# Mixture of experts on one core: one-hot rows from PSUM for seven experts, an expert's outputs ahead of the slot numbers three experts on

## The chip, the cores and the metric

The kernel runs on one core of a Trainium2 chip. The metric is the device time of one execution in microseconds (us); less is better. Compared are medians of several executions.

## The reference

The input `x` is 2 x 2048 tokens of 256 numbers. Four blocks follow each other, each a layer norm, a layer and a residual sum:

```
x = x + linear_attention(layernorm(x))      # 16 heads of 16
x = x + ffn(layernorm(x))                   # mixture of 8 experts
x = x + windowed_attention(layernorm(x))    # causal, a window per head, gates
x = x + ffn(layernorm(x))                   # the same weights once more
```

The change lies in `ffn`, which is computed twice:

```
probs = softmax(xf @ gate_w.T)              # 4096 tokens x 8 experts
scores = route(probs)                       # threshold 0.9, then the best 512 tokens of each expert
y = sum over e of scores[:, e] * (gelu(xf @ w1[e].T) @ w2[e].T)
```

Each expert keeps at most 512 tokens, so the kernel computes an expert on 512 gathered rows alone.

## The kernel before

Tokens lie in 32 tiles of 128. While the attention blocks run, `router` writes every normalized row and its 8 probabilities to DRAM (`rows_a`, and `rows_b` in the second pass) and the running sum `x` to `mid` (in the second pass `out_rows`). Then `experts` works alone on the core, once behind each attention.

`experts` first finds each expert's threshold by bisection. Then it gives each kept token a slot. A slot's number is split into a part `hi` (which of 128 rows) and a part `lo` (which of four blocks). For an expert `e` four steps turn this into token numbers:

- `columns_of(e)`: two small VectorE (DVE) products (L1013 into `olo`, L1017 into `olw`) and one on ScalarE (ACT, L1016 into `olw`).
- `rows_of(e)`: two one-hot tiles `ohi` of 16 token tiles x 128, one a half. For `e < SHARED` both operands are bf16 in SBUF (L1028, with `hi2` written by L1078); for other experts the counting numbers are fp32 in PSUM (`iota_ps`, L1034).
- `tokens(e)`: 32 small matmuls on TensorE (PE, L1045) sum `ohi` against `olw` into `w_ps`, 16 for each half; then three small DVE steps (L1049, L1050, L1052) write the token numbers `idx[e]`.
- `gather(n)`: the next `n` blocks of 128 rows are fetched by indirect DMAs that GpSimd (POOL) issues (L1070, into `xe`).

The loop over experts (L1097) then does for `e`: eight transposes of the four blocks on PE (`transposed`, L247), two copies of the result to SBUF (ACT L251; the second on DVE, L249), the first product (`h_ps`, L1110, 8 matmul records), Gelu on ACT (L1112), and for each of the four blocks the second product (`y_ps`, L1123, in two PSUM buffers), its scaling on DVE (L1126 into `y`) and an indirect DMA on POOL that adds 128 rows into `mid` or `out_rows` (L1127). Inside the loop also stand `columns_of`, `rows_of` and `tokens` of expert `e + 3`: between the Gelu and the second product.

PE, ACT and DVE work through their instructions in the order in which the code is written. POOL's order is fixed by dependencies: gathers in their order, an expert's additions behind the last gather written before them (`follow`), gathers behind the additions written before them. An expert's additions also wait until those of the expert before have landed. The `gather` tuple at the end of the loop says how many blocks are fetched behind each expert's additions; together with `gather(2)` for `e == 0` all 32 blocks are fetched. SyncE (SP) has no transfer in this loop. `xe` has four buffers, `ohi` four, `y` eight.

Of the kernel before, what the change touches and what calls it, by code (L numbers as in the profile page):

```python
# [30 lines left out]
E, F = 8, 256  # L31
# [23 lines left out]
CENTERS, SCALES = (-6.0, -3.0, -1.5, -0.5), (0.25, 0.5, 1.0, 1.0)  # L55
STEPS = [0.25 * 4.0**-i for i in range(12)]
SIGN = 2.0**20
SHARED = 3
ROUND = 1.5 * 2.0**23 * GT


# [73 lines left out]
def hybrid_kernel(ctx: ExitStack, tc: tile.TileContext, x, wq, wk, wv, wo, wqk, bqk, wgate, bgate, wproj, bproj,  # L135
# [13 lines left out]
    def part(t, name):  # L149
        o, n = at[name]  # L150
        return t[:, o : o + n]
# [9 lines left out]
    def con(name):  # L161
        return part(cst, name)
# [78 lines left out]
    def transposed(pool, psum, xn, copies=None, n=GT):  # L241

        xnT = pool.tile([P, NC, GW], F32, name="xnT", tag="xnT")[:, :, 0 : n * P]
        for c in range(NC):
            pt = psum.tile([P, GW], F32, name="xnT_ps", tag="mm")[:, 0 : n * P]
            for i in range(n):
                nc.tensor.transpose(pt[:, i * P : (i + 1) * P], xn[:, i, c * P : (c + 1) * P], ident)  # L247
            if c and copies is None:
                nc.vector.tensor_copy(xnT[:, c, :], pt)  # L249
            else:  # L250
                nc.scalar.copy(xnT[:, c, :], pt)  # L251
        return xnT
# [640 lines left out]
    def experts(acc, name, rows, scores):  # L893
        score, over = scores
        with ExitStack() as st:
            pool = st.enter_context(tc.tile_pool(name=f"mx_{name}", bufs=2))
            one = st.enter_context(tc.tile_pool(name=f"mo_{name}", bufs=1))
            mm = st.enter_context(tc.tile_pool(name=f"mm_{name}", bufs=4, space=PSUM))
# [98 lines left out]
            hi = one.tile([P, E, NT], BF16, name="hi")  # L997
            hi2 = one.tile([P, SHARED, NT, 2], BF16, name="hi2")
            lo = one.tile([P, E, NT], BF16, name="lo")

            def of(t, e):
                return t.rearrange("p (t e) -> p e t", e=E)[:, e]
# [7 lines left out]
            def columns_of(e):  # L1010

                olo = pool.tile([P, NT, GT], BF16, name="olo", tag="olo")
                nc.vector.tensor_tensor(olo, lo[:, e].unsqueeze(2).to_broadcast([P, NT, GT]),  # L1013
                                        part(sel, "places").unsqueeze(1).to_broadcast([P, NT, GT]), ALU.is_equal)
                columns[e] = olw = pool.tile([P, NT, 2, GT], BF16, name="olw", tag="olw")
                nc.scalar.activation(olw[:, :, 0, :], olo, AF.Copy, scale=con("within"))  # L1016
                nc.vector.tensor_tensor(olw[:, :, 1, :], olo, part(sel, "tile").rearrange("p (t l) -> p t l", l=GT),  # L1017
                                        ALU.mult)
# [3 lines left out]
            def rows_of(e, halves=range(2)):  # L1022

                for b in halves:
                    ohi = pool.tile([P, half, P], BF16, name="ohi", tag="ohi", bufs=4)
                    at_b = slice(b * half, (b + 1) * half)
                    if e < SHARED:
                        nc.vector.tensor_tensor(  # L1028
                            ohi.rearrange("p t (a b) -> p t a b", b=2),
                            hi2[:, e, at_b].unsqueeze(2).to_broadcast([P, half, P // 2, 2]),  # L1030
                            iota.rearrange("p (a b) -> p a b", b=2).unsqueeze(1).to_broadcast([P, half, P // 2, 2]),
                            ALU.is_equal)
                    else:
                        nc.vector.tensor_tensor(ohi, iota_ps.unsqueeze(1).to_broadcast([P, half, P]),  # L1034
                                                hi[:, e, at_b].unsqueeze(2).to_broadcast([P, half, P]), ALU.is_equal)
                    ones.setdefault(e, []).append(ohi)

            def tokens(e):

                olw = columns.pop(e)  # L1040
                w_ps = sm.tile([P, 2, GT], F32, name="w_ps", tag="sm")
                for b, ohi in enumerate(ones.pop(e)):
                    for t in range(half):
                        n = b * half + t
                        nc.tensor.matmul(w_ps.rearrange("p w l -> p (w l)"), ohi[:, t, :],  # L1045
                                         olw[:, n].rearrange("p w l -> p (w l)"), start=(n == 0), stop=(n == NT - 1))

                row = pool.tile([P, GT], F32, name="row", tag="row")
                nc.vector.scalar_tensor_tensor(row, w_ps[:, 0, :], 0.0, con("spare"), ALU.is_equal, ALU.mult)  # L1049
                nc.vector.scalar_tensor_tensor(row, w_ps[:, 0, :], -1.0, row, ALU.add, ALU.add)  # L1050
                idx[e] = one.tile([P, GT], I32, name=f"idx{e}")
                nc.vector.scalar_tensor_tensor(idx[e], w_ps[:, 1, :], float(P), row, ALU.mult, ALU.add)  # L1052
# [12 lines left out]
            def gather(n):  # L1065

                for e, b in blocks[:n]:
                    if b == 0:
                        xes[e] = pool.tile([P, GT, XR], F32, name="xe", tag="xe", bufs=4)
                    read = nc.gpsimd.indirect_dma_start(  # L1070
                        out=xes[e][:, b, :], out_offset=None, in_=rows[:, :],
                        in_offset=bass.IndirectOffsetOnAxis(ap=idx[e][:, b : b + 1], axis=0))
                    follow(read, reads[-1:] + added)
                    reads.append(read)
                del blocks[:n]

            for e in range(SHARED):
                nc.vector.tensor_scalar(hi2[:, e], of(up, e).unsqueeze(2).to_broadcast([P, NT, 2]), ROUND, 1.0 / GT, ALU.subtract,  # L1078
# [10 lines left out]
            for e in range(1, 3):  # L1089
# [3 lines left out]
                    los(slice(2, E))  # L1093
                tokens(e)
                gather(GT)
            columns_of(3)
            for e in range(E):  # L1097
                xe = xes.pop(e)
                adds = []

                for blocks_in in ((range(GT),) if e + 1 < E else (range(GT - 1), range(GT - 1, GT))):
                    at0, n = blocks_in[0], len(blocks_in)
                    xT = transposed(pool, mm, xe[:, at0 : at0 + n, :], None, n)
                    if e == 0:
                        rows_of(3)
                    hT = pool.tile([P, F // P, GW], F32, name="hT", tag="hT")
                    for f in range(F // P):
                        h_ps = mm.tile([P, GW], F32, name="h_ps", tag="mm")
                        for c in range(NC):
                            nc.tensor.matmul(h_ps[:, 0 : n * P], w1_sb[:, e, c, f * P : (f + 1) * P], xT[:, c, :],  # L1110
                                             start=(c == 0), stop=(c == NC - 1))
                        nc.scalar.activation(hT[:, f, 0 : n * P], h_ps[:, 0 : n * P], AF.Gelu)  # L1112
                    if e + 3 < E:
                        if e:
                            columns_of(e + 3)
                            rows_of(e + 3)
                        tokens(e + 3)
                        if e == 0:
                            gather(2)
                    for b in blocks_in:  # L1120
                        y_ps = yp.tile([P, D], F32, name="y_ps", tag="y")
                        for f in range(F // P):
                            nc.tensor.matmul(y_ps, hT[:, f, (b - at0) * P : (b - at0 + 1) * P], w2_sb[:, e, f, :],  # L1123
                                             start=(f == 0), stop=(f == F // P - 1))
                        y = pool.tile([P, D], F32, name="y", tag="y", bufs=8)
                        nc.vector.tensor_scalar(y, y_ps, xe[:, b, D + e : D + e + 1], None, ALU.mult)  # L1126
                        add = nc.gpsimd.indirect_dma_start(  # L1127
                            out=acc[:, :], out_offset=bass.IndirectOffsetOnAxis(ap=idx[e][:, b : b + 1], axis=0),
                            in_=y, in_offset=None, compute_op=ALU.add)

                        for other in adds:
                            tc.declare_no_dep(add.ins, other.ins, reason="rows of one expert's slots differ")
                        for other in added:
                            tc.add_manual_dep(add.ins, other.ins.name, landed, reason="sums of the expert before")
                        follow(add, reads[-1:])
                        adds.append(add)
                added = adds
                gather((2, 3, 3, 3, 3, 3, 1, 0)[e])
            return added


# [585 lines left out]
```

## Time and profile before

| what | value |
|---|---|
| median of 11 executions | 907.49 us (903.46 to 909.62) |
| the profiled execution | 907.75 us |
| its span, first to last instruction | 905.6 us |
| mean granted TensorE clock | 0.913 |
| busy, whole span | PE 84%, DVE 72%, POOL 48%, ACT 43% |
| expert loop, first pass | first gather at 331.79 us, end of the last addition's issue at 443.0 us |
| expert loop, second pass | first gather at 789.65 us, end of the last addition's issue at 901.15 us |

The profile is one execution. Times in its rows count from the first instruction. A timeline row has the start, the duration, the engine (PEld is the weight load of PE), the source line, the operation, the tiles written and read, how many instructions are merged, and in brackets how long the engine was idle before and what ended the idle time. A row of stretches has the length, the busy time of each engine with its number of instructions, the granted TensorE clock, the DMA engines' share and GB/s. A row of instruction groups has the line, the operation, the shapes, the count, then busy time and mean nanoseconds, then idle time before. A row of waits has who waited for whom, the total, the number of times, and the longest.

### The profile page before, as it was taken

Reading aid. Unit: us, or ns where it says so; the run is one execution under the profiler, and the core shown is the slowest. Engines: PE = TensorE matmul, PEld = TensorE weight load, DVE = VectorE, ACT = ScalarE, POOL = GpSimd, SP = SyncE. Lnnn points to the kernel's source line nnn. Section 1 sums busy time; section 2 is a strip of 40 time slices with the busy share of each in tenths; the row PEclk is TensorE's granted clock in tenths of the full one; section 3 lists DMA queues with packets and bytes.
Section 4 is the critical chain, followed back from the end, with each engine's and each line's share of the span. In section 5 each row is a group of like instructions: output and inputs, shape, how many; then the busy total and the mean of one; then the engine's idle time right before and its main releaser. Section 6 shows DMA issues by size and latency. Waiting matters only on the chain.

```text
span 905.6 us, 17491 instructions
## 1 busy us (share of the span) xinstructions
PE 756.5 (84%) x6520; PEld 503.7 (56%) x6520; DVE 649.0 (72%) x1665; ACT 387.5 (43%) x1117; POOL 438.7 (48%) x506
## 2 busy tenths in 40 slices
PE   8999999999999327887588999999999993268785
PEld 5577677676677214554345666665656662145453
DVE  6778778678668776652369898888988887856621
ACT  3545545544444331111145576665665762411111
POOL 1233325235235126778543655563655442157786
PEclk8999999999999557999799999999999996569987
DMA  9830101101102113545662023123031212025554
GB/s 310 234 109 6 49 3 47 48 1 49 49 1 96 29 28 74 77 74 81 122 178 63 27 60 109 49 60 105 14 102 56 54 60 65 7 78 77 78 77 63
DMA packets 63996, 65.01 MB, mean 72 GB/s; under 512 B 7244, under 2 KB 60521, under 8 KB 63913
## 3 DMA queue, kind: packets, MB, share of 16 engines
q1 hardware_dynamic: 49945, 44.66, 16.2%
q0 software_dynamic: 12992, 18.42, 12.6%
q8 instruction: 51, 0.84, 0.4%
q10 hardware_dynamic: 976, 0.84, 0.3%
q14 instruction: 32, 0.26, 0.1%
HBM read 26.47 MB, written 27.56 MB: 60 GB/s over the span
## 4 chain that ended last, share of the span: by engine, by line
PE 22%; DVE 18%; issue 4%; ACT 3%; POOL 3%; DMA 1%; POOLq 0%; SPq 0%; DVEq 0%; ACTq 0%
PE tk_ps L1197 5%; PE y_ps L1123 3%; PE wo_ps L1430 2%; PE xnT_ps L247 2%; DVE ohi L1034 2%; PE pt_ps L1395 2%; POOL out_rows L1127 2%; DVE ln_stats L218 2%; DVE wa_xn L226 2%; PE pj_ps L1452 1%; DVE og L1325 1%; DVE s L1287 1%; PE wqk_ps L1204 1%; ACT wpr L1386 1%; PE sa_ps L1365 1%
## 5 line engine op out<-in xcount | busy, mean ns | idle before, releaser
L251 ACT COPY xnT<-xnT_ps 128x512 f32<-128x512 f32 (+2 forms) x73 | 39.0, 563 | 125.9 <-PE xnT_ps L247 125.9
L223 POOL TENSOR_TENSOR ln_rstd<-ln_rstd,cst_parts 128x4 f32<-128x4 f32 (+3 forms) x35 | 34.7, 992 | 114.3 <-DVE ln_rstd L222 77.2
L1123 PE MATMUL y_ps<-w_sb,hT 128*128 128x256 f32 x256 | 69.7, 421 | 7.2 <-DVE y L1126 5.7
L1110 PE MATMUL h_ps<-xnT,w_sb 128*128 128x512 f32 (+2 forms) x144 | 67.3, 615 | 9.8 <-ACT xnT L251 9.3
L1126 DVE TENSOR_SCALAR y<-y_ps,xe 128x256 f32<-128x256 f32 x64 | 30.5, 483 | 58.9 <-PE y_ps L1123 54.7
L523 POOL TENSOR_TENSOR a_sb<-a_raw,cst_first 128x512 f32<-128x512 f32 x32 | 41.1, 1284 | 60.8 <-ACT a_raw L522 60.8
L525 DVE TENSOR_TENSOR a_sb<-s_ps,cst_first 128x512 f32<-128x512 f32 x96 | 60.0, 680 | 8.0 <-PE s_ps L511 8.0
L1123 PEld LDWEIGHTS y_ps<-w_sb,hT 128*128 128x128 f32 x256 | 50.3, 208 | 23.1 <-DVE y L1126 8.9
L218 DVE BATCH_NORM_STATS2 ln_stats<-x 128x6 f32<-128x256 f32 x128 | 53.4, 417 | 7.1 <-DMA x<-in_x 3.3
L1397 ACT COPY pt<-pt_ps 128x256 f32<-128x256 f32 (+3 forms) x94 | 42.0, 468 | 37.1 <-PE pt_ps L1395 36.7
L1127 POOL DMA_INDIRECT out_rows<-y,idx x32 | 50.6, 1582 | 14.9 <-issue 6.6
L1127 POOL DMA_INDIRECT mid<-y,idx x32 | 50.4, 1576 | 14.5 <-DVE y L1126 6.5
L1197 PE MATMUL tk_ps<-wt_sb,xnT 128*128 128x432 f32 x128 | 52.8, 539 | 0.5 <-ACT xnT L251 0.5
L1070 POOL DMA_INDIRECT xe<-rows_a,idx x32 | 31.4, 981 | 41.1 <-DVE idx L1052 29.9
L1070 POOL DMA_INDIRECT xe<-rows_b,idx x32 | 31.3, 978 | 41.1 <-DVE idx L1052 29.9
L1110 PEld LDWEIGHTS h_ps<-xnT,w_sb 128*128 128x128 f32 x144 | 27.9, 211 | 40.5 <-issue 22.7
L1386 ACT ACTIVATE wpr<-sn_ps,negm 128x128 f32<-128x128 f32 x128 | 45.8, 375 | 0.0
L1395 PE MATMUL pt_ps<-cst_parts,wpr 128*128 128x128 f32 x280 | 44.3, 282 | 1.3 <-ACT wpr L1386 1.0
L1112 ACT ACTIVATE hT<-h_ps 128x512 f32<-128x512 f32 (+2 forms) x36 | 19.8, 550 | 59.0 <-PE h_ps L1110 58.9
L1034 DVE TENSOR_TENSOR ohi<-iota_ps,hi 128x2048 bf16<-128x2048 f32 x20 | 44.8, 2280 | 0.0
L1395 PEld LDWEIGHTS pt_ps<-cst_parts,wpr 128*128 128x128 f32 x280 | 31.1, 140 | 24.2 <-issue 5.6
L1045 PE MATMUL w_ps<-olw,ohi 128*128 128x8 bf16 x512 | 17.7, 167 | 31.0 <-DVE ohi L1028 13.6
(260 smaller groups left out, 2097.1 us busy)
## 6 DMA issues: line engine op xcount, KB each, us to landing
ks<-tk SPq DMA_DIRECT2D x21, 280.0 KB
rows_a<-xr SPq DMA_DIRECT2D x7, 528.0 KB
rows_b<-xr SPq DMA_DIRECT2D x7, 528.0 KB
x<-in_x SPq DMA_DIRECT2D x7, 512.0 KB
mid<-x SPq DMA_DIRECT2D x7, 512.0 KB
x<-mid SPq DMA_DIRECT2D x7, 512.0 KB
out_rows<-x SPq DMA_DIRECT2D x7, 512.0 KB
w_sb<-in_w1t SPq DMA_DIRECT2D x1, 2048.0 KB
```

Of the source, the lines that this page charges most:

```text
L218: nc.vector.bn_stats(self.stats[:, i, :], self.xin[:, i, :])
L523: nc.gpsimd.tensor_tensor(a, raw, causal, ALU.mult)
L525: nc.vector.tensor_tensor(a, s_ps[j], causal, ALU.mult)
L1034: nc.vector.tensor_tensor(ohi, iota_ps.unsqueeze(1).to_broadcast([P, half, P]), hi[:, e, at_b].unsqueeze(2).to_broadcast([P, half, P]), AL ...
L1070: read = nc.gpsimd.indirect_dma_start(out=xes[e][:, b, :], out_offset=None, in_=rows[:, :], in_offset=bass.IndirectOffsetOnAxis(ap=idx[e][ ...
L1110: nc.tensor.matmul(h_ps[:, 0 : n * P], w1_sb[:, e, c, f * P : (f + 1) * P], xT[:, c, :], start=(c == 0), stop=(c == NC - 1))
L1123: nc.tensor.matmul(y_ps, hT[:, f, (b - at0) * P : (b - at0 + 1) * P], w2_sb[:, e, f, :], start=(f == 0), stop=(f == F // P - 1))
L1127: add = nc.gpsimd.indirect_dma_start(out=acc[:, :], out_offset=bass.IndirectOffsetOnAxis(ap=idx[e][:, b : b + 1], axis=0), in_=y, in_offse ...
L1197: nc.tensor.matmul(ps, self.xnT[:, c, i * P : (i + 1) * P], wt_sb[:, c, :], start=(c == 0), stop=(c == NC - 1))
L1386: nc.scalar.activation(self.pr[:, o : o + w], src, AF.Exp, bias=self.negm[:, h : h + 1], accum_out=self.den[:, h : h + 1])
L1395: nc.tensor.transpose(ps[:, n, :], self.pr[:, (o + n) * P : (o + n + 1) * P], ident)
L1397: (nc.vector.tensor_copy if engine else nc.scalar.copy)(pt[:, skip:w, :], ps[:, skip:w, :])
```

## The change

Three things are edited. `SHARED` falls from 3 to 1: `hi2` and the bf16 form of `rows_of` stay for expert 0 alone. `columns_of(3)` leaves the place ahead of the loop and `rows_of(3)` and `tokens(3)` the middle of expert 0: all three stand behind expert 0's additions, and expert 0's second copy of the transposed rows goes from DVE to ACT. For later experts `columns_of(e + 3)` and the first half of `rows_of(e + 3)` stand ahead of the first product, and the second half and `tokens(e + 3)` behind the additions of `e`. `gather(2)` inside expert 0 is gone: its additions stand behind the first twelve gathers, and four gathers follow them in place of two.

```diff
-SHARED = 3
+SHARED = 1
...
-            columns_of(3)
             for e in range(E):
                 xe = xes.pop(e)
                 adds = []
 
                 for blocks_in in ((range(GT),) if e + 1 < E else (range(GT - 1), range(GT - 1, GT))):
                     at0, n = blocks_in[0], len(blocks_in)
-                    xT = transposed(pool, mm, xe[:, at0 : at0 + n, :], None, n)
-                    if e == 0:
-                        rows_of(3)
+                    xT = transposed(pool, mm, xe[:, at0 : at0 + n, :], None if e else "scalar", n)
+                    ahead = e + 3 if e + 3 < E else None
+                    if ahead and e:
+                        columns_of(ahead)
+                        rows_of(ahead, [0])
...
                         nc.scalar.activation(hT[:, f, 0 : n * P], h_ps[:, 0 : n * P], AF.Gelu)
-                    if e + 3 < E:
-                        if e:
-                            columns_of(e + 3)
-                            rows_of(e + 3)
-                        tokens(e + 3)
-                        if e == 0:
-                            gather(2)
                     for b in blocks_in:
...
                 added = adds
-                gather((2, 3, 3, 3, 3, 3, 1, 0)[e])
+                if ahead:
+                    if e == 0:
+                        columns_of(ahead)
+                    rows_of(ahead, range(2) if e == 0 else [1])
+                    tokens(ahead)
+                gather((4, 3, 3, 3, 3, 3, 1, 0)[e])
```

## The prediction, made before the changed kernel was run

> **What bounds the kernel now.** I read the page for where the experts lie, then the stretches of the expert loop, POOL's waits, the timeline, and last the clock by window. All numbers are of the first pass; the second repeats it within a microsecond (the loop takes 111.2 and 111.5 us). The stretches are cut where an expert's first addition begins, the last two here those of experts 3 and 4:
>
> ```profile
> 365.30:377.90 12.60, 10.08 (x65) 6.58 (x65) 8.17 (x13) 2.07 (x4) 9.23 (x7) 0.95 0.52 85
> 377.90:390.50 12.60, 11.02 (x65) 7.05 (x65) 7.90 (x13) 2.07 (x4) 9.30 (x8) 0.86 0.49 75
> 390.50:402.80 12.30, 9.49 (x65) 6.18 (x65) 7.79 (x13) 2.07 (x4) 9.26 (x7) 1.00 0.50 75
> 402.80:414.20 11.40, 10.32 (x42) 6.73 (x41) 3.74 (x8) 1.78 (x3) 9.23 (x8) 1.00 0.51 72
> ```
>
> POOL is busy 9.3 us of each, and every one of its issues is followed by 0.30 us, so seven take 11.4 us: experts 4 to 6 run at POOL's own pace. Experts 1 to 3 take 12.3 to 12.6, because POOL waits for `y`:
>
> ```profile
> POOL mid L1127 <- DVE y L1126: 6.5, 6, 1.7
> ```
>
> The timeline has an expert without number work (expert 5), which gives the bare chain, and the release of expert 0's additions:
>
> ```profile
> 345.19 5.81 PE L1110 MATMUL h_ps<-xnT,w_sb 128*128 128x512 f32 x8 [2.61 <-ACT xnT L251]
> 352.64 0.95 POOL L1070 DMA_INDIRECT xe<-rows_a,idx  x1 [3.71 <-DVE idx L1052]
> 355.38 0.48 DVE L1126 TENSOR_SCALAR y<-y_ps,xe 128x256 f32<-128x256 f32 x1 [0.38 <-issue]
> 355.17 1.04 PE L247 MATMUL xnT_ps<-cst_parts,xe 128*128 128x128 f32 x8
> 404.44 1.04 PE L247 MATMUL xnT_ps<-cst_parts,xe 128*128 128x128 f32 x8
> 410.90 0.48 DVE L1126 TENSOR_SCALAR y<-y_ps,xe 128x256 f32<-128x256 f32 x1 [4.62 <-PE y_ps L1123]
> 413.49 0.48 DVE L1126 TENSOR_SCALAR y<-y_ps,xe 128x256 f32<-128x256 f32 x1 [0.38 <-DMA xe<-rows_a,idx]
> ```
>
> To be seen: from the first transpose to the end of the first `y` 6.94 us, to the end of the last 9.53. Expert 1's transposes start (355.17) before expert 0's last `y` is done, since expert 3's one-hot rows were made beside expert 0's `h`.
>
> **The change part by part.** The DVE's groups price the rows:
>
> ```profile
> L1034 DVE TENSOR_TENSOR ohi<-iota_ps,hi 128x2048 bf16<-128x2048 f32 x10 | 22.4, 2280 | 0.0
> L1028 DVE TENSOR_TENSOR ohi<-hi,cst_sel 128x2048 bf16<-128x2048 bf16 x6 | 7.1, 1217 | 0.0
> ```
>
> *SHARED 3 to 1.* Experts 1 and 2 get a pair of 4.47 us (two of 2.28, overlapping) in place of 2.35: +2.12 each; the two `hi2` steps go (-0.2). Expert 1's pair runs 332.13 to 336.60; 0.6 for 16 matmuls and 0.55 for three small steps give `idx` at 337.8, against 337.32 before. That is only +0.5, because before DVE read `w_ps` 1.4 us after the modelled end of its matmuls (2.6 us for expert 2), while for expert 0 it was 0.04. Expert 2's pair then ends at 342.8, its matmuls at 343.4, and expert 0's transposes follow at half clock (four of 0.215 and 0.3): copy 344.55 to 345.1, `h` at 345.2. Before it was 345.19, since the copies stood behind `idx` and `columns_of(3)`. I take 0. Bounds: +2.6 if the late reading is added again; -2.0 if the clock, now fed by transposes right ahead of `h`, rises one 3.41 us window earlier than at 349.46. The middle of this last, -1.0, goes into expert 0 below.
>
> *Both copies on ACT for expert 0:* nothing; ACT is idle there, and the second copy ends at 346.0, before its matmul at 346.9. Without that slack it costs its own 0.58. *ACT's `olw` ahead of Gelu:* nothing; `olo` is there 2.1 us behind the transposes, `olw` at 2.55, the first `h` at 3.4. DVE's first half (2.28) lies under `h` and ends 1.7 us before `y`.
>
> *Expert 0's additions behind twelve gathers.* POOL waited until 352.64 for expert 3's numbers and put two gathers ahead of the additions (355.14). Now the additions start with `y`, at about 353.5, and all four gathers come behind them. The sum of POOL's work is the same, and the 1.6 us are lost again if the numbers come late, and they do.
>
> *Expert 3's numbers behind expert 0's outputs.* DVE's last `y` ended at 355.86; it is not sooner for want of `w_ps`, because `y` also waits for Gelu (351.63); less the 1.0 above it is 354.9. Then 0.5 (`olo`, `olw`), 4.47 (the pair), 0.6 (matmuls): expert 1's transposes, behind them on PE, start at 360.5 in place of 355.17. POOL has issued expert 0's four additions (7.5) by then and its gathers wait for `idx`, with expert 1's additions queued behind. Expert 1's first addition comes 7.2 after its transposes (6.94 and 0.26 to POOL): 367.7, against 365.34.
>
> *The second half behind `y`.* For experts 1 to 4 a period is now 9.53 to the last `y`, 2.28 for the half, 0.6 for 16 matmuls, then the next transposes: 12.4 us. Before, both halves stood in the same chain, partly under `h`, at 12.0 to 12.6. So the moved work frees POOL's wait for `y`, but puts its price between two experts. No DMA is moved but the gathers, and SP has none here. POOL's 11.4 fits into the period: it is no longer the pace.
>
> *The clock.* PE's gap per expert is now in one piece: from the last `y_ps` (8.85 behind the transposes) to 12.4, 3.5 us with only 32 tiny matmuls in it. Such a gap decides the clock (its column is the third from the end):
>
> ```profile
> 359.70:363.11 3.41, 2.25 (x38) 1.68 (x37) 2.58 (x4) 0.89 (x2) 2.80 (x3) 1.00 0.59 69
> 363.11:366.53 3.42, 3.42 (x10) 2.71 (x9) 0.97 (x2) 0.00 (x0) 2.75 (x3) 0.50 0.54 118
> 397.25:400.66 3.41, 2.31 (x38) 2.09 (x38) 1.58 (x1) 0.84 (x2) 2.50 (x4) 1.00 0.55 91
> 400.66:404.07 3.41, 2.08 (x10) 1.50 (x9) 1.60 (x6) 0.00 (x0) 2.17 (x2) 1.00 0.32 79
> ```
>
> A window with 2.25 us of modelled PE time, half of it the tiny matmuls, was followed by half clock for 3.41 us, one with 2.31 was not. A window with 3.5 us of gap in or around it lies well below both, so I take one cold window in nearly every period from expert 1 to 5. It begins in the gap and covers about 2.2 us of the next transposes and `h`, which run at half speed: +1.1 us (bounds 0.5 to 1.7, a window less its part in the gap, halved).
>
> [...]
>
> *Sum for a pass.* Expert 1's first addition: 367.7 + 1.2 = 368.9. Four periods of 12.4 + 1.1: expert 5's at 422.9, against 414.20: +8.7. From there both kernels have POOL's pace (11.4), and expert 7's first addition waits 4.6 us for the landing of expert 6's last (issued 431.27, next 435.87), so the end moves with expert 5: +8.7. Two passes: +17.4 us on the profiled 907.75, which lies 0.26 above the median: 925.
>
> **The rivals.** *Warm clock:* the same chain without cold windows. Expert 1 at 367.7, expert 5 at 367.7 + 4 x 12.4 = 417.3: +3.1 a pass, 914. For it: POOL's idle before shows only some experts with a cold window. Against: the longer gap.
>
> *Faster, POOL set free:* the gain that `y` ahead of the numbers could have. If POOL never waits for `y`, experts 1 to 5 follow at 11.4: 365.3 + 4 x 11.4 = 410.9 against 414.2, -3.3 a pass, 901. It decides only if expert 1's transposes start by 358.1 (365.34 - 7.2), that is 2.2 us behind expert 0's last `y`, where the pair alone takes 4.47; and if a period then falls to 11.4, where the chain has 12.4.
>
> *No difference:* POOL covers all of it, because the two kernels' periods are alike (12.4 and 12.5) and expert 1 comes in time: 907.5. The 5.3 us of expert 1 speak against it.
>
> *Colder:* late reading at the start (transposes of expert 1 at 362.0), four windows of 3.41 in a period (13.65), one more cold window of 1.5 behind: 362.0 + 8.4 + 54.6 = 425.0, +10.8, and 1.5: +12.3 a pass, 932.
>
> **How the numbers follow.** Forecast (cold, 925) 0.63; warm (914) 0.20; colder (932) 0.10; faster (901) 0.04; none 0.03. Low end: warm clock and the clock's early rise in full (expert 1's transposes at 359.4, expert 5 at 416.2): +2.0 a pass, 911.7. High end: the colder case, 932. Outside lie the faster, the unchanged, and part of the colder and warm cases. About 0.2% (1.8 us) is what a measurement of this kernel can tell from no change: faster 0.04, within 0.03, slower 0.93.
>
> **What would show each step.** Right: in the timeline expert 1's transposes at about 360 behind `w_ps`, DVE's pair between expert 0's last `y` and them; 13 to 14 us between first additions of experts 1 to 5 and POOL waiting for `y` 2 us each time; granted clock in the loop well below 0.86; `h` at 345 as before. Wrong: expert 1's transposes before 358; `w_ps` L1045 not waiting for `ohi` L1034; POOL without idle time between experts; or a period of 12.4 at full clock, which gives the warm case.

## The result and the profile after

The kernel after takes 928.5 us (median of 12 runs, 925.7 to 931.5), the kernel before beside it 906.5 us (46 runs): 2.4% slower, ratio 1.0241 with a 95% interval of 1.0225 to 1.0257. The forecast was 925.0, its range 911.7 to 932.0. The profiled executions took 931.9 and 907.75 us.

Nearly all of it lies in the two expert loops. From the start of the first gather to the end of the last addition's issue the first pass takes 122.4 us (before 111.2), the second 121.9 (before 111.5): 21.5 us of the 24.2 by which the two profiled executions differ (the medians differ by 22.0). The stretches of the first pass, cut where an expert's first addition begins (experts 1 to 4; columns as in the prediction's first fence, the third from the end is the granted clock):

```profile
370.57:384.46 13.89, 10.95 (x66) 6.71 (x65) 7.94 (x12) 2.18 (x4) 9.25 (x7) 0.88 0.44 68
384.46:398.24 13.78, 10.84 (x66) 6.72 (x65) 7.94 (x12) 2.18 (x4) 9.26 (x7) 0.88 0.44 69
398.24:411.95 13.71, 10.77 (x66) 6.71 (x65) 7.93 (x12) 2.18 (x4) 9.28 (x7) 0.88 0.44 68
411.95:425.64 13.69, 10.78 (x66) 6.68 (x65) 5.30 (x9) 1.78 (x3) 9.25 (x8) 0.88 0.46 69
```

POOL's work is the same 9.25 us, but a period is 13.7 to 13.9 us in place of 11.4 to 12.6, and the clock is 0.88 in each of them. The chain of waits (total, times, longest) gives what POOL waits for; it was 6.5 us in 6 waits before:

```profile
POOL mid L1121 <- DVE y L1120: 18.8, 7, 4.0
```

The timeline has expert 0 and the step to expert 1. (The file is a little shorter: `h_ps` is now L1111, `y_ps` L1117, `y` L1120, the additions L1121.)

```profile
345.38 5.77 PE L1111 MATMUL h_ps<-xnT,w_sb 128*128 128x512 f32 x8
...
353.34 1.63 POOL L1121 DMA_INDIRECT mid<-y,idx  x1 [4.01 <-DVE y L1120]
...
355.16 0.48 DVE L1120 TENSOR_SCALAR y<-y_ps,xe 128x256 f32<-128x256 f32 x1 [0.38 <-PE y_ps L1117]
...
356.02 4.48 DVE L1034 TENSOR_TENSOR ohi<-iota_ps,hi 128x2048 bf16<-128x2048 f32 x2
...
360.56 0.59 PE L1045 MATMUL w_ps<-olw,ohi 128*128 128x8 bf16 x16 [1.64 <-DVE ohi L1034]
361.01 1.95 PE L247 MATMUL xnT_ps<-cst_parts,xe 128*128 128x128 f32 x8
...
370.57 1.62 POOL L1121 DMA_INDIRECT mid<-y,idx  x1 [3.74 <-DVE y L1120]
...
375.55 1.07 PE L247 MATMUL xnT_ps<-cst_parts,xe 128*128 128x128 f32 x8
...
376.92 5.36 PE L1111 MATMUL h_ps<-xnT,w_sb 128*128 128x512 f32 x8 [0.29 <-ACT xnT L251]
```

Expert 3's pair of one-hot rows stands alone between expert 0's last `y` (355.16) and expert 1's transposes (361.01, before 355.17). DVE's groups in the loop's stretch have the one-hot rows of the other price, 14 of 2.28 us and two of 1.22 where there were ten and six:

```profile
L1034 DVE TENSOR_TENSOR ohi<-iota_ps,hi 128x2048 bf16<-128x2048 f32 x14 | 31.7, 2281 | 0.0
L1028 DVE TENSOR_TENSOR ohi<-hi,cst_sel 128x2048 bf16<-128x2048 bf16 x2 | 2.4, 1222 | 0.0
```

In the timeline expert 1's transposes take 1.95 us in place of 1.04: the clock is at half (0.50 in the windows below). POOL's additions wait 3.74 us. Expert 2's transposes (375.55, 1.07 us) run at nearly full clock; its `h`, from 376.92 on, begins at half. The clock by window:

```profile
359.81:363.22 3.41, 2.66 (x25) 2.44 (x26) 1.40 (x5) 0.59 (x1) 1.79 (x2) 0.50 0.52 67
363.22:366.64 3.42, 3.42 (x5) 1.34 (x5) 3.09 (x4) 0.44 (x2) 2.69 (x3) 0.50 0.38 106
373.46:376.88 3.42, 1.49 (x24) 1.25 (x24) 2.26 (x5) 0.59 (x1) 2.81 (x3) 1.00 0.60 68
376.88:380.29 3.41, 3.38 (x4) 1.52 (x5) 3.16 (x4) 0.40 (x1) 2.80 (x3) 0.50 0.68 100
387.12:390.53 3.41, 1.49 (x24) 1.25 (x24) 2.34 (x4) 0.36 (x1) 2.80 (x3) 1.00 0.62 73
390.53:393.94 3.41, 3.13 (x4) 1.52 (x5) 3.28 (x4) 0.63 (x2) 2.80 (x3) 0.50 0.65 89
```

A window with 1.49 us of PE time is followed by one at half clock, in both periods shown. The first column gives the spacing: cold windows begin at 376.88 and 390.53, 13.65 us apart, which is four windows of 3.41, and the period closes in on that from 13.89 to 13.69.

### The profile page after: what moved, and what is told of

The parts are those of the page before. It is cut to its first block, busy times and chain, and to the rows that moved or that the text cites. A ratio compares the mean times of both kernels' runs of the same rounds, so it can differ in the third digit from the quotient of the medians.

```text
span 930.1 us, 17467 instructions
## 1 busy us (share of the span) xinstructions
PE 770.3 (83%) x6520; PEld 508.5 (55%) x6520; DVE 654.7 (70%) x1659; ACT 390.7 (42%) x1119; POOL 438.7 (47%) x506
## 4 chain that ended last, share of the span: by engine, by line
PE 26%; DVE 15%; ACT 4%; issue 3%; POOL 2%; DMA 1%; SPq 0%; POOLq 0%; DVEq 0%; ACTq 0%
PE tk_ps L1196 5%; PE h_ps L1111 4%; PE y_ps L1117 2%; PE wo_ps L1429 2%; DVE ohi L1034 2%; PE pt_ps L1394 2%; PE xnT_ps L247 2%; PE wqk_ps L1203 2%; PE pj_ps L1451 2%; DVE ln_stats L218 1%; DVE og L1324 1%; PE sa_ps L1364 1%; PE sn_ps L1362 1%; ACT wpr L1385 1%; POOL out_rows L1121 1%
## 5 line engine op out<-in xcount | busy, mean ns | idle before, releaser
L1120 DVE TENSOR_SCALAR y<-y_ps,xe 128x256 f32<-128x256 f32 x64 | 31.0, 484 | 97.1 <-PE y_ps L1117 96.0
L251 ACT COPY xnT<-xnT_ps 128x512 f32<-128x512 f32 (+3 forms) x75 | 40.2, 565 | 137.9 <-PE xnT_ps L247 137.8
L1111 PE MATMUL h_ps<-xnT,w_sb 128*128 128x512 f32 (+2 forms) x144 | 80.7, 717 | 4.0 <-ACT xnT L251 4.0
L1117 PE MATMUL y_ps<-w_sb,hT 128*128 128x256 f32 x256 | 64.2, 393 | 3.9 <-ACT hT L1113 3.6
L1121 POOL DMA_INDIRECT mid<-y,idx x32 | 50.4, 1576 | 27.8 <-DVE y L1120 18.8
L1121 POOL DMA_INDIRECT out_rows<-y,idx x32 | 50.6, 1580 | 27.5 <-DVE y L1120 18.4
L1034 DVE TENSOR_TENSOR ohi<-iota_ps,hi 128x2048 bf16<-128x2048 f32 x28 | 63.4, 2281 | 0.0
L1117 PEld LDWEIGHTS y_ps<-w_sb,hT 128*128 128x128 f32 x256 | 46.2, 193 | 24.7 <-ACT hT L1113 10.8
L1111 PEld LDWEIGHTS h_ps<-xnT,w_sb 128*128 128x128 f32 x144 | 33.8, 257 | 41.7 <-issue 25.1
L1045 PEld LDWEIGHTS <-ohi 128*128 128x128 bf16 x512 | 16.3, 100 | 59.8 <-DVE ohi L1034 51.6
```

The source lines that it names most:

```text
L1121: add = nc.gpsimd.indirect_dma_start(out=acc[:, :], out_offset=bass.IndirectOffsetOnAxis(ap=idx[e][:, b : b + 1], axis=0), in_=y, in_offse ...
```

## The experiments

**What they are to tell apart.** My theory after the result: the loss is expert 3's exposed number work behind expert 0, the half of the rows behind `y`, and one cold window a period; the first part (`SHARED`) costs next to nothing. The rivals: the longer one-hot rows are the loss; the clock follows the gap without costing anything; the place of the gathers is the loss.

**How to read the numbers.** The kernels came in groups, each group on one chip with the kernel before beside it. The kernel before took 906.5 us beside the first result and 894.1, 906.3, 894.5 and 901.3 us in the four groups, which were on four different chips. So every kernel is given against the kernel before of its own group. That these places differ turned out to be part of the answer. Differences in us are between medians; a ratio and its interval are an estimate over all runs, and with few runs the two can disagree: e0_only is 11.7 us slower by the medians, and 10 us by its ratio of 1.011. "Loop" is, as above, one pass from the first gather to the end of the last addition's issue; "first additions" are counted from the first gather.

### First group (the kernel before: 894.1 us)

**s1_only**, the first part alone:

```diff
-SHARED = 3
+SHARED = 1
```

> The kernel before with the first part of the change alone (one-hot rows of experts 1 and 2 with numbers in PSUM). My theory, in which the loss lies in the loop's order and in the clock: the start-up absorbs it, expert 0's first h within 0.5 us of 345.2 and the periods unchanged, 0 to +2 us a pass, 906 to 910. Rival, the longer one-hot rows are the loss: +10 a pass, about 927.

Measured 901.5 us, +7.4 (1.0091, interval 1.0069 to 1.0114). My "0 to +2 a pass" failed: it is 3.7 a pass. The periods (11.4) are POOL's own; the cost is at the start. Ahead of the loop, in the timelines of the kernel before (first profile), of gathers_only and of s1_only:

```profile
334.74 0.59 PE L1045 MATMUL w_ps<-olw,ohi 128*128 128x8 bf16 x16 [0.54 <-issue]
...
336.77 0.16 DVE L1049 SCALAR_TENSOR_TENSOR row<-w_ps,cst_parts 128x4 f32<-128x4 f32 x1 [1.68 <-PE w_ps L1045]
```

```profile
334.05 0.59 PE L1045 MATMUL w_ps<-olw,ohi 128*128 128x8 bf16 x16 [0.55 <-DVE ohi L1028]
334.68 0.16 DVE L1049 SCALAR_TENSOR_TENSOR row<-w_ps,cst_parts 128x4 f32<-128x4 f32 x1 [0.27 <-PE w_ps L1045]
```

```profile
336.11 0.59 PE L1045 MATMUL w_ps<-olw,ohi 128*128 128x8 bf16 x16 [1.61 <-DVE ohi L1034]
336.74 0.16 DVE L1049 SCALAR_TENSOR_TENSOR row<-w_ps,cst_parts 128x4 f32<-128x4 f32 x1 [0.27 <-PE w_ps L1045]
```

With the same bf16 rows, the kernel before of the first profile reads `w_ps` 1.44 us behind the end of the matmuls (336.77), gathers_only of this group at once (334.68). So the late reading, by which I had costed `SHARED` at nothing, is absent here, and nearly the full price of the longer pairs (2 x 2.1 us a pass, against 3.7 measured) is seen.

**s3_after**, the kernel after with that part undone (`SHARED = 3`):

> The kernel after with the first part undone (bf16 one-hot rows for experts 1 and 2 again), the order of the loop as changed. My theory: almost nothing comes back, 0 to 4 us in all, 925 to 928.5, expert 1's first addition at about 370 and periods of 13.7 as in the kernel after. Rival, the one-hot rows are the loss: back to about 907.

Measured 918.6 us, +24.5 (1.0283, interval 1.0260 to 1.0306). The periods are 13.6 to 13.8, as in the kernel after: the order of the loop carries most of the loss. Against the kernel after of a later group where the kernel before took the same time (after_3, +33.1) `SHARED` is worth 8.6 us, near s1_only's 7.4 and more than the 0 to 4 I had allowed.

**warm_gap**, the kernel after with unused matmuls in PE's gap:

```diff
+                    if e:
+                        warm(mm, w2_sb[:, e, 0, :], 4)
                     tokens(ahead)
```

> The kernel after with four more matmuls (128x256, some 1.7 us at full clock, their products unused) on PE ahead of each number step of experts 1 to 4, where PE has its gap. My theory, in which cold clock windows make 1.3 us of each of four periods: the clock stays full in the loop, periods go from 13.7 to about 12.4, -5 us a pass, about 918. Rival, the clock only follows the gap and costs nothing: 928.5, or later by the matmuls' own time if they delay the 32 number matmuls.

Measured 917.3 us, +23.2 (1.0259, interval 1.0233 to 1.0284). Seven of the eight periods in two passes fell to between 12.1 and 12.4; the one from expert 4 to 5 in the first pass stayed at 13.93. The total could not be judged without the kernel after in the same group; it was run again below.

**gathers_only**, the third part alone:

```diff
-                        if e == 0:
-                            gather(2)
...
-                gather((2, 3, 3, 3, 3, 3, 1, 0)[e])
+                gather((4, 3, 3, 3, 3, 3, 1, 0)[e])
```

> The kernel before with the third part alone: expert 3's first two gathers no longer ahead of expert 0's additions, all four behind them. My theory: expert 0's additions start about 2 us earlier, POOL's sum of work up to expert 1's additions is the same, so -1 to +2 us a pass, 905 to 911. Rival, that the gathers' place makes the loss (expert 3's tokens come late): expert 3's transposes wait, over +5 us a pass, 917 or more.

Measured 895.2 us, +1.0 (1.0014, interval 1.0001 to 1.0027). The place of the gathers is not the loss. Its first addition comes 16.8 us behind the first gather, but expert 1's at 29.5, the periods behind it are 11.4, and the loop is 103.8. The stretches of experts 1 and 2:

```profile
360.57:371.94 11.37, 9.87 (x70) 6.54 (x68) 8.22 (x13) 2.44 (x5) 9.23 (x7) 1.00 0.55 84
371.94:383.33 11.39, 9.45 (x64) 6.12 (x64) 8.04 (x13) 2.25 (x5) 9.26 (x8) 1.00 0.55 82
```

A kernel with the numbers in the order of before can therefore run at POOL's pace throughout.

### Second group (the kernel before: 906.3 us)

**before_2** and **after_2**, both kernels once more for their profiles:

> The kernel before once more, for its profile beside the kernels of this call. In the profile shown first DVE read w_ps 1.4 to 2.7 us behind the matmuls for most experts; in the kernels with part of the change run since, it read at once and experts 1 to 4 followed at 11.4 us. If late reading belongs to that place of measurement and not to the kernel: here it is prompt, periods of 11.4, loop about 105 us a pass instead of 111. Rival, it belongs to the kernel before's order: late again, periods 12.5, loop 111.

> The kernel after once more, beside the kernel before of this call. My theory: its periods of 13.7 are four clock windows and its reading of w_ps was prompt already, so its loop stays at about 122 us a pass, and where the kernel before takes 105 the loss is larger than measured first, over +25 us in all, ratio about 1.03. Rival, the place of measurement moves both alike: the loss stays at 22 us, ratio 1.024.

before_2 took 904.3 us, with loops of 108.7 and 110.8 and again late readings (1.7 to 2.2 us for experts 5 to 7). That alone fits the rival, that lateness belongs to the order of before; but gathers_only and s1_only, whose experts 5 to 7 are handled as in before, read at once in the first group. So the order alone does not make a reading late. Nor do gathers beside the number matmuls: in the kernel after, in a place where the kernel before reads late, expert 1's and 2's numbers ahead of the loop run beside gathers too, and are read 0.07 and 0.06 us behind. Expert 1's in the kernel after (first profile):

```profile
336.05 0.95 POOL L1070 DMA_INDIRECT xe<-rows_a,idx  x1 [0.30 <-issue]
...
336.96 0.59 PE L1045 MATMUL w_ps<-olw,ohi 128*128 128x8 bf16 x16 [1.61 <-DVE ohi L1034]
337.62 0.16 DVE L1049 SCALAR_TENSOR_TENSOR row<-w_ps,cst_parts 128x4 f32<-128x4 f32 x1 [0.31 <-PE w_ps L1045]
```

There the two halves of the matmuls lie 2.2 us apart. In the first profile of the kernel before, the late readings (1.4 to 2.7 us) have the halves 0.7 or 1.1 us apart and gathers beside them; expert 4's, with 0.7 us and no gather beside it, is read at once (0.03 us), but 0.31 us late in before_2. So gathers alone do not make a reading late, and what does no run shows.

after_2 took 927.9 us, +21.6 (1.0242, interval 1.0203 to 1.0281), its loops 120.4 and 121.0, all its readings prompt (at most 0.08 us). The first measurement repeats.

**later_only**, expert 0 as before, the changed order for experts 1 to 4:

```diff
+            columns_of(3)
...
+                    if e == 0:
+                        rows_of(3)
...
+                    if e == 0:
+                        tokens(3)
+                        gather(2)
...
-                if ahead:
-                    if e == 0:
-                        columns_of(ahead)
-                    rows_of(ahead, range(2) if e == 0 else [1])
+                if ahead and e:
+                    rows_of(ahead, [1])
                     tokens(ahead)
-                gather((4, 3, 3, 3, 3, 3, 1, 0)[e])
+                gather((2, 3, 3, 3, 3, 3, 1, 0)[e])
```

(and `SHARED = 3`, ACT's second copy back on DVE; the diff is against the kernel after.)

> The changed order for experts 1 to 4 alone; expert 0 (numbers of expert 3 beside its h, two gathers ahead of its additions) and the bf16 one-hot rows as before. My theory: expert 1's first addition comes as in the kernel before, then four periods of 13.65 by the clock in place of 11.4 to 12.5: +5 to +9 us a pass. Rival, expert 0's part is the loss: periods stay at POOL's 11.4 and the time is that of the kernel before.

Measured 911.8 us, +5.5 (1.0052, interval 1.0031 to 1.0073): 2.8 us a pass, where I had expected 5 to 9. Its stretches from expert 0's first addition on show why (experts 0, 1 and 3):

```profile
353.51:364.03 10.52, 8.68 (x48) 5.45 (x46) 6.95 (x10) 2.18 (x4) 8.32 (x7) 1.00 0.54 78
364.03:375.39 11.36, 10.06 (x49) 6.62 (x50) 6.24 (x11) 2.18 (x4) 9.23 (x7) 0.85 0.53 83
...
387.20:400.68 13.48, 10.83 (x66) 7.02 (x65) 8.00 (x12) 2.18 (x4) 9.27 (x7) 0.87 0.49 78
```

The chain has a lead on POOL when it enters expert 1, since expert 1's transposes ran early. The 13.5 us of the new order show only when that lead is used up, from expert 2 or 3 on.

**e0_only**, the changed order for expert 0 alone:

```diff
-            columns_of(3)
...
-                    if e == 0:
-                        rows_of(3)
...
-                    if e + 3 < E:
-                        if e:
-                            columns_of(e + 3)
-                            rows_of(e + 3)
+                    if e and e + 3 < E:
+                        columns_of(e + 3)
+                        rows_of(e + 3)
                         tokens(e + 3)
-                        if e == 0:
-                            gather(2)
...
+                if e == 0:
+                    columns_of(3)
+                    rows_of(3)
+                    tokens(3)
+                gather((4, 3, 3, 3, 3, 3, 1, 0)[e])
```

(against the kernel before, with ACT's second copy for expert 0.)

> The changed order for expert 0 alone (its outputs ahead of expert 3's numbers, all four gathers behind its additions); experts 1 to 4 and the bf16 one-hot rows as before. My theory: expert 1's first addition comes about 17 us behind expert 0's instead of 10 to 13, then POOL's own pace of 11.4: 0 to +4 us a pass by how far POOL catches up. Rival, expert 0's part carries the whole loss: +10 us a pass.

Measured 918.0 us, +11.7 (1.011, interval 1.006 to 1.016), more than the +4 a pass I had allowed, though not the whole 21.6. Its stretches of experts 0 and 1:

```profile
351.56:369.95 18.39, 12.54 (x98) 8.25 (x97) 13.24 (x19) 2.47 (x5) 10.21 (x8) 0.81 0.37 59
369.95:382.51 12.56, 9.51 (x66) 6.14 (x65) 8.20 (x13) 2.07 (x4) 9.23 (x7) 1.00 0.49 76
```

Expert 1's first addition comes 18.4 us behind expert 0's (10.5 in before_2), 38.1 us behind the first gather in place of 31.6. I had expected POOL to catch up at 11.4; the periods of experts 1 to 3 stay at 12.3 to 12.6, for the numbers of experts 5 to 7 are read 2.0 to 2.1 us late here too, and the delay goes through to the end.

e0_only also tells why `SHARED` did cost nothing in this place. It has bf16 rows for experts 1 and 2, which after_2 has not. Expert 0's first additions come 19.7 us (first pass) and 21.6 us (second) behind the first gather, those of after_2 20.2 and 20.7. What the shorter rows save, 2 x 2.1 us, is lost to late readings of 1.47 us (expert 1) and 2.63 us (expert 2).

### Third and fourth group (the kernel before: 894.5, then 901.3 us)

**warm_gap_2** and **after_3** in one group:

> The kernel after with four unused matmuls in PE's gap, once more, now beside the kernel after itself in one call. My theory: periods of 12.24 instead of 13.65, 4 x 1.4 = 5.6 us a pass, so 11 us (9 to 12) under the kernel after. Rival, the first comparison, in which it stood 2.6% above the kernel before, is the whole truth and the clock gives nothing: equal to the kernel after.

> The kernel after, as a partner for warm_gap_2 and to see whether the loss depends on how promptly w_ps is read by the kernel before in this place: ratio 1.024 where the kernel before takes 906, over 1.03 where it takes 894.

after_3 took 927.6 us, +33.1 (1.0362, interval 1.0343 to 1.0381); warm_gap_2 took 916.6 us, +22.1 (1.0245, interval 1.0223 to 1.0267). They differ by 11.0 us. Stretches, first of after_3 (experts 1 to 3), then of warm_gap_2 (experts 1 to 4):

```profile
367.67:381.17 13.50, 10.85 (x66) 6.79 (x65) 7.93 (x12) 2.18 (x4) 9.29 (x7) 0.87 0.46 70
381.17:394.75 13.58, 10.88 (x66) 6.66 (x65) 7.93 (x12) 2.18 (x4) 9.26 (x7) 0.87 0.47 70
394.75:408.37 13.62, 10.85 (x66) 6.64 (x65) 7.93 (x12) 2.18 (x4) 9.28 (x8) 0.87 0.46 68
```

```profile
369.29:381.53 12.24, 11.02 (x74) 7.59 (x73) 7.93 (x12) 2.18 (x4) 9.24 (x7) 1.00 0.51 75
381.53:393.76 12.23, 11.01 (x74) 7.58 (x73) 7.93 (x12) 2.18 (x4) 9.26 (x7) 1.00 0.51 76
393.76:406.00 12.24, 11.02 (x74) 7.59 (x73) 7.94 (x12) 2.18 (x4) 9.28 (x7) 1.00 0.50 76
406.00:419.93 13.93, 12.71 (x74) 8.17 (x73) 5.31 (x9) 1.78 (x3) 9.24 (x7) 0.88 0.46 71
```

With eight records more on PE the period is 1.3 us shorter at full clock: the gap costs through the clock. In the last row the filled gap did not help. Two windows of warm_gap_2 show it:

```profile
409.23:412.64 3.41, 2.45 (x43) 2.00 (x42) 2.25 (x5) 0.59 (x1) 2.80 (x3) 1.00 0.61 63
412.64:416.05 3.41, 3.41 (x5) 1.35 (x5) 0.21 (x1) 0.07 (x1) 2.57 (x3) 0.50 0.61 94
```

A window with 2.45 us of PE time was followed by half clock, although one with 2.31 in the kernel before was not; PE's busy time alone does not decide. So the 11.0 us are not eight periods of 1.4. In the two profiles the loops differ by 2.8 us in the first pass (119.2 against 116.4) and 5.4 in the second (121.9 against 116.5), together 8.2. The rest lies outside the loops, where both kernels have the same code: between the two loops alone the profiles differ by 3.6 us (349.3 against 345.7). The clock's part in the loops is thus about 8 us.

And after_3 settles the other point: the median of the kernel after was 927.6 to 928.5 us each of the three times, so the size of the loss, 22 or 33 us, is set by the kernel before.

**read_behind**, the order of before with DVE's reading of the numbers behind `y` and expert 3's first two gathers behind expert 0's additions, as a way to beat both:

```diff
-                        tokens(e + 3)
-                        if e == 0:
-                            gather(2)
+                        tokens(e + 3, False)
...
                 added = adds
-                gather((2, 3, 3, 3, 3, 3, 1, 0)[e])
+                if e + 3 < E:
+                    numbers(e + 3)
+                gather((4, 3, 3, 3, 3, 3, 1, 0)[e])
```

(`tokens(e, False)` issues the matmuls alone; `numbers(e)` is the three DVE steps to `idx`.)

> The kernel before with only DVE's reading of w_ps (three small steps to idx) moved behind the y of the same pass of the loop, and expert 3's first two gathers behind expert 0's additions; rows and the 32 number matmuls stay ahead of y. My theory: where the kernel before reads w_ps late, y stands behind that wait on DVE; here POOL never waits, periods of 11.4 for experts 1 to 4 and the first addition no later, 104 to 106 us a pass instead of 111, -10 to -14 us in all; where reading is prompt anyway, -1 to +2 us. Rival, the chain of rows, matmuls and y sets 12.4 whatever the reading does: no change.

> The kernel with DVE's reading of w_ps behind y once more, for a place where the kernel before reads late. My theory: there the loop takes 104 to 106 us a pass instead of 109 to 111 and the kernel stands 10 to 14 us under the kernel before (about 894 to its 906). Rival: late reading costs through something else (the numbers come late to POOL too), so less than 4 us. Where the kernel before reads promptly (894): no difference, as measured already, and the question stays open.

Measured 895.4 us in the third group, +1.0 (1.0006, interval 0.9992 to 1.0021): no difference, as expected where reading is prompt. In the fourth, on another chip, read_behind_2 took 904.7 us, +3.4 (1.0035, interval 1.0019 to 1.0051), where I had hoped for -10 at a late place: a miss. (The kernel before has no profile there; the place is a late one by this run's own numbers of experts 1 and 2, read 0.68 and 0.60 us behind.) An expert's numbers and first `y`, first in read_behind, then in read_behind_2 (`w_ps` is L1047, `y` L1133, the addition L1134):

```profile
369.63 0.56 PE L1047 MATMUL w_ps<-olw,ohi 128*128 128x8 bf16 x16 [0.20 <-DVE ohi L1034]
...
371.20 0.48 DVE L1133 TENSOR_SCALAR y<-y_ps,xe 128x256 f32<-128x256 f32 x1 [1.62 <-PE y_ps L1130]
```

```profile
373.40 0.56 PE L1047 MATMUL w_ps<-olw,ohi 128*128 128x8 bf16 x16 [0.48 <-issue]
...
375.95 0.87 DVE L1133 TENSOR_SCALAR y<-y_ps,xe 128x256 f32<-128x256 f32 x2 [2.61 <-PE y_ps L1130]
...
376.71 1.62 POOL L1134 DMA_INDIRECT mid<-y,idx  x1 [1.38 <-DVE y L1133]
```

From the second half of the number matmuls to the first `y` it is 1.57 us in the one and 2.55 in the other, and in the other two `y` follow each other at once. So it isn't DVE's early reading that makes `y` late: here what PE hands over behind the number matmuls is itself late. The periods of experts 1 to 3 are 12.45 in the first pass, where read_behind has 11.4. No version here beat the kernel before.

## Why the prediction was right, point by point

- *`SHARED` at nothing*: right in its place (`h` of expert 0 at 345.38, before 345.19), for the reason given, the late reading. But that reason is not the kernel's own: it holds where the kernel before takes 906. Where it takes 894 the part costs 7.4 us alone, 8.6 in the new order. That the result was measured in such a place was luck. The early rise of the clock, half counted at -1.0, did not come in the profiled execution: last `y` of expert 0 ends at 355.64, not 354.9. It did come in part in after_2: `h` of expert 0 took 5.77 us here and 4.73 there.
- *What bounds the kernel before*: the prediction put its 12.0 to 12.6 us down to the rows and numbers that stand in one chain with `y`. With this order of the numbers the periods are 11.4 in s1_only and gathers_only, so the excess belongs to the late readings. The comparison came out because it was measured where these occur: the forecast was 17.4 us over the kernel before, which is 22.0 and 21.6 where it takes 906 and 33.1 where it takes 894.
- *Expert 0's additions with `y`*: forecast 353.5, measured 353.34. The 1.6 us won are lost again as said: POOL waits 1.44 us for expert 3's `idx`.
- *Expert 1*: transposes forecast at 360.5, measured 361.01; first addition 368.9 against 370.57. The clock is cold for two windows here (359.81 to 366.64), where the sum has one (1.2 us); warm_gap_2 adds no matmuls in this gap, so their price was not measured by itself. In after_2 expert 1's first addition stands at 332.28 + 36.92 = 369.2.
- *The period*: the warm one, 12.4, is borne out by 12.24 in warm_gap_2. The cold window was sized +1.1; it is 1.4 (13.65 - 12.24). The window does not begin in the gap, as the prediction had it, with 2.2 us of it over PE's work. It begins behind the next transposes (375.55, the window at 376.88), and PE is busy for 3.38 of its 3.41 us. That the period closes in on whole windows was only in the rival "colder", whose late reading at the start did not come. With 13.8 in place of 13.5, four periods make 1.1 us of the miss, expert 1's 1.7 the rest: expert 5 at 425.64, not 422.9.
- *The clock as a sign*: "well below 0.86" was wrong; it is 0.88 in every period. One window of four at half speed makes 0.875, so the prediction's own cold window could not give less.
- *The tail*: unchanged as said, 28.8 us from expert 5's first addition to the end of the loop in both profiles. So a pass takes longer by 11.2 and 10.4 us instead of 8.7; the median came out 3.5 above the forecast.
- *The rivals*: warm and cold were 11 us apart in the forecast (914 and 925) and are 11.0 us apart in warm_gap_2 and after_3, but only about 8 of these lie in the loops, so the agreement is in part luck. "POOL set free" needed expert 1's transposes by 358.1 and a period of 11.4; neither occurred. "Warm clock" needed full clock in the periods; it was 0.88 in the kernel after, where windows with 1.49 us of PE work in 3.41 were followed by half clock, as one with 2.45 was in warm_gap_2.

Where reading is prompt the parts nearly add up. `SHARED` 8.6; the clock 11.0 by the medians; the half of the rows behind `y` 2 x 4 x (12.24 - 11.39) = 6.8; expert 0's part, by expert 1's first additions in s3_after against gathers_only, 3.1 + 4.3 = 7.4. Together 33.8, against 32.1 between after_3 (+33.1) and gathers_only (+1.0). Part of this agreement is luck too: the 11.0 holds some 3 us from outside the loops, and the 6.8 takes eight periods of 12.24, of which one was 13.93. Where it is late, expert 0's part (11.7) and the later experts' (5.5) leave 4.4 of 21.6. The interval of e0_only alone (1.006 to 1.016) is 4.5 us to either side, so the remainder may be nothing. If it is real, I put it down to POOL's lead, which hides the first long periods of later_only and which expert 0's part takes away; that is argued from the stretches, not run by itself.

## What to carry to other kernels

The work that moved off POOL's wait for `y` into PE's gap was paid there twice here: with its own time (periods of 12.24 us at full clock, where gathers_only has 11.39), and with the clock (13.65 in place of 12.24). The gap left windows partly empty, and over the profiles here windows with 1.49, 2.25 and 2.45 us of PE work in 3.41 were followed by half clock, one with 2.31 was not. Price such a gap by the windows of the profile, and ask whether the period will settle on whole windows, as it did here (four of 3.41, 13.65). Before a step is costed at nothing because "the consumer is late anyway", ask what makes it late: here it held in some places (expert 1's numbers 1.44 us late in the first profile) and not in others (0.04 in gathers_only). And take the parts of a reordering one by one from both ends, since a lead of one engine can hide in one part what another part uses up.

## What the runs showed of the hardware that was not expected

- The same kernel takes 906 us beside the first result and on the chip of the second group, 901 on that of the fourth, 894 on those of the first and third. In its profiles where it takes 906, most number matmuls are handed over late, by 1.4 to 2.7 us in the first profile and 0.3 to 2.7 in before_2; in the kernels profiled where it takes 894, PE hands over at once (expert 1's numbers 0.04 us behind in s1_only and gathers_only). In the first profile of the kernel before, where it is late, PE's semaphore events come in a bunch: six lie between 343.39 and 343.59, for expert 2's number matmuls and expert 0's transposes, which were issued from 340.63 on; in gathers_only the same six spread from 338.62 to 340.42, in the kernel after from 343.78 to 345.57. The ends of matmuls are modelled in the profile, so PE itself may have been held. What holds it or its events back was not found.
- In the kernel after all readings are prompt (0.03 to 0.08 us), also those ahead of the loop that have gathers beside them, and its median lies within 1 us (927.6 to 928.5) the three times it was measured.
- The loop of the kernel after, with one cold window a period, closes in on four windows, 13.65 us, whether expert 1 began early or late: in the first pass from 13.50 up to 13.63 in after_3, from 13.89 down to 13.69 in the first profile.
